# A selective scan's units in a new order: five pairs of states by tokens, three by rows, and the carry by DMA

## The chip, the cores and the metric

The kernel runs on one core of a Trainium2 chip. A NeuronCore has four engines that compute, each with its own instruction stream: TensorE (PE) for matrix products, VectorE (DVE), ScalarE (ACT) and GpSimd (POOL). A fifth, SyncE (SP), only issues DMAs. They meet through semaphores. The metric is the device time of one execution in microseconds; lower is better. Unless another length is named, a "group" and a "unit" below are those of the second layer's scan.

## The reference, cut to what matters

Two layers of a state-space image model on 64 x 64 positions with 96 channels, each `x + conv_ref(groupnorm(x))`. The change lies in the second layer, in its selective scan: 4 directions, 192 inner channels, 16 states, 4096 positions.

```python
A = -jnp.exp(A_logs)
def step(h, t):
    u_t, d_t, B_t, C_t = t
    h = h * jnp.exp(d_t[..., None] * A[None]) + (d_t * u_t)[..., None] * B_t[:, :, None, :]
    y = jnp.einsum('bkdn,bkn->bkd', h, C_t)
    return (h, y)
```

For every channel d and state n this is a first-order recurrence along the positions: a = exp(dt x A), b = dt x u x B, h = a x h + b, and y sums h x C over the states. Before it stand projections, a depthwise convolution and a softplus for dt; after it a layer norm, a gate and an output projection.

## The kernel before, in words

**Groups.** Layer 2's scan is the function `scans`. Its work is cut into 16 groups: two pairings of directions, two directions, four chunks of 1024 positions. A group needs `dt` and `du` (dt times u) of its chunk, B and C.

**Units.** A group has 24 units: three blocks T of 64 channels by eight pairs m of states. A tile of a unit has 128 partitions (two states by 64 channels) and 1024 positions. A unit goes through these steps, each a small function:

- `stage_a` (ScalarE): a = exp(dt x A), into a pool of three buffers
- b, in PSUM, in one of two ways. By rows: `stage_B` (TensorE) spreads two rows of B over the partitions by two matmuls, and `stage_b` (VectorE) multiplies the result by `du`. By tokens: ScalarE has multiplied `du`, transposed so that positions lie on partitions, by B as a scale for each partition (`product`, 16 operations for a pair m, shared by the three T, into seven buffers `bT`); `stage_t` (TensorE) turns the products back with eight transposes, and VectorE has nothing to multiply
- `stage_s` (VectorE): the scan itself, one instruction, into `h`, a pool of three buffers
- `stage_k`: the last element of each partition of h is copied to `carry`, from which the next chunk's unit starts. It is left out for a direction's last chunk
- `stage_c` (GpSimd): hc = h x C; C's two rows come from DRAM, spread over 64 partitions each by two DMAs into `cb` (`fetch_c`, three buffers)
- `stage_r` (TensorE): sums hc over the states into PSUM, on top of y; `stage_y` (ScalarE) copies y out after the last pair

Before the change the even pairs go by rows and the odd by tokens, and the units alternate: row unit, token unit, row unit. The row units' b lies in PSUM tile `b0`, the token units' in `b1`.

**The order.** The last loop of `scans` writes the program out unit by unit. In its iteration j it emits b of unit j+1, a of unit j+2, the product b x du and the scan of unit j, the sum of unit j-3, carry and C product of unit j-1. Everything emitted through `pe`, `act`, `dve`, `pool` and `sp` keeps this order on its engine. Tiles are handed over by semaphores: whoever writes a buffer again waits for its last reader.

**Preludes.** What group k+1 needs is made while group k runs, by the list `steps`: each entry has a slot (a unit's number, counted from the group's own start, so slots below 0 lie in the group before) and is emitted at the end of the iteration that the slot falls in. `delta(T)` is the softplus for dt (ten steps), `project`, `first_part`, `less_part`, `next_part`, `rows` and `tokens_B` make B and C, `tokens_du` transposes du, `spread(T)` copies dt and du to both halves of the partitions with eight DMAs on SP. `turns` says how many of the 16 products of each token pair are emitted in which unit.

**SP's queue** carries, in program order: the DMAs of `fetch_c`, `spread` and `rows`. Each of its DMAs signals one of eight semaphores in turn, and an issue waits until the DMA eight issues earlier has landed.

In the profile all instructions that go through `Ordered` have the line of its `issue` (L653 before), so they are told apart by their tiles.

Of the kernel before, what the change touches and what calls it, by code (L numbers as in the profile page):

```python
# [8 lines left out]
F32 = mybir.dt.float32  # L9
# [12 lines left out]
NP = NS // 2  # L22
RK = 6
TC = 1024
# [19 lines left out]
def two_ss2d_layers(  # L44
# [592 lines left out]
    def scans(weights):  # L637

        xw, dwb, _ = weights
        pinned = []

# [16 lines left out]
        with ExitStack() as sc:  # L661
# [5 lines left out]
            am = decays(weights[2])  # L667
            carry = pre.tile([128, 3, NP], F32, name="carry")
            PER = 3 * NP
            LAG = 3  # L670
            halves = [slice(0, HT), slice(HT, TC)]
            state = [{} for _ in GROUPS]
# [24 lines left out]
            def prelude(k):  # L697
# [81 lines left out]
                def delta(T):  # L779

                    def begin():
                        ps = me["pd", T] = spare(f"pd{k}_{T}", tags[2 + T])
                        for h, half in enumerate(HALF):
                            pe.matmul(
                                ps[half], dwb[p][96 : NC + 1, d, T, half],
                                xd[96 : NC + 1, halves[h]], start=True, stop=True,
                            )

                    def new(nm, own):
                        t = me[nm, T] = pre.tile(  # L790
                            [128, HT], F32, tag=f"{nm}{T}" if own else nm, name=f"{nm}{k}_{T}"
                        )
                        return t

                    def absolute():
                        act.activation(new("su", True), me["pd", T], AF.Abs)

                    def positive():
                        act.activation(new("sp", True), me["pd", T], AF.Relu)

                    def exponent():
                        act.activation(new("w", False), me["su", T], AF.Exp, scale=-1.0)

                    def logarithm():
                        act.activation(new("ln", False), me["w", T], AF.Ln, bias=one)

                    def plus():
                        act.activation(me["pd", T], me["w", T], AF.Identity, bias=one)

                    def missed():  # L810

                        dve.scalar_tensor_tensor(
                            me["w", T], me.pop(("pd", T)), -1.0, me["w", T], ALU.add, ALU.subtract
                        )

                    def found():
                        add_engine.tensor_sub(me["ln", T], me["ln", T], me["w", T])

                    def whole():
                        add_engine.tensor_add(me["sp", T], me["sp", T], me["ln", T])  # L820

                    def times():
                        add_engine.tensor_mul(me["su", T], me["sp", T], chunk(u[T], c))

                    return [
                        begin, absolute, positive, exponent, logarithm, plus, missed,
                        found, whole, times,
                    ]

                def spread(T):  # L830
                    for nm, of in (("dt", "sp"), ("du", "su")):
                        t = me[nm, T] = pre.tile(
                            [128, TC], F32, tag=f"{nm}{T}", name=f"{nm}{k}_{T}"
                        )
                        both(t.rearrange("p (h t) -> p h t", h=2), me[of, T], sp)
# [4 lines left out]
                for h in range(2):  # L840
# [10 lines left out]
                        (o + 3 + late, lambda h=h: next_part(1, h)),  # L851
                    ]
                steps += [
                    (-9, rows), (-6.8, tokens_B), (-5.95, tokens_B_out),

                    *zip((-1.5, -1, -1, 0, 1, 1, 2, 3, 4, 5), delta(0)),
                    *zip((2.5, 3, 3, 4, 5, 5, 6, 7, 8, 9), delta(1)),
                    *zip((6.5, 7, 7, 8, 9, 9, 10, 11, 12, 13), delta(2)),
                ]
                steps += [(18.5 + e, lambda e=e: tokens_du(e)) for e in range(4)]  # L860
                steps += [(19 + e, lambda e=e: tokens_du_out(e)) for e in range(4)]
                steps += [(18 + 2 * T, lambda T=T: spread(T)) for T in range(3)]


                turns = (
                    (19, (4, 4, 4, 4)), (PER, (3, 1, 5, 1, 3, 3)), (PER + 6, (4, 2, 3, 1, 3, 3)),
                    (PER + 12, (2, 3, 3, 2, 3, 3)),
                )
                for i, (slot, counts) in enumerate(turns):
                    todo = [(e, h, n) for e in range(4) for h in range(2) for n in range(2)]  # L870
# [8 lines left out]
            def product(k, i, e, h, n):  # L879


                me = state[k]
                if (h, n) == (0, 0):
                    me["bT", i, e] = mn.tile(
                        [128, 2, 3, 2, 64], F32, tag="bT", name=f"bT{k}_{i}{e}", bufs=7
                    )
                q = 2 * (2 * i + 1) + n
                act.mul(
                    me["bT", i, e][:, h, :, n, :], me["duT", e][:, h],
                    me["BT"][:, e + 4 * h, q : q + 1],  # L890
                )

            units = [
                (k, T, 2 * i + odd)
                for k in range(len(GROUPS)) for i in range(NP // 2) for T in range(3)
                for odd in range(2)
            ]
            N = len(units)
            live = {}

# [8 lines left out]
            def stage_B(j):  # L909

                k, T, m = units[j]
                ps = live["b", j] = pps.tile([128, TC], F32, tag="b0", name=f"b{j}")
                for s in halves:
                    pe.matmul(
                        ps[:, s], pick(GROUPS[k][1], m), state[k]["B3"][:, s], start=True, stop=True
                    )

            def stage_t(j):

                k, T, m = units[j]  # L920
                ps = live["b", j] = pps.tile([128, TC], F32, tag="b1", name=f"b{j}")
                for e in range(4):
                    t = state[k]["bT", m // 2, e]
                    for h in range(2):
                        q = e + 4 * h
                        pe.transpose(
                            ps[:, 128 * q : 128 * (q + 1)],
                            t[:, h, T].rearrange("p n c -> p (n c)"), ident,
                        )
# [23 lines left out]
            def stage_k(j):  # L953
                k, T, m = units[j]
                p, d, c = GROUPS[k]
                if c != (NCH - 1 if d == 0 else 0):
                    act.copy(carry[:, T, m : m + 1], along(d, live["h", j])[:, TC - 1 : TC])

            def stage_c(j):
                k, T, m = units[j]  # L960
# [3 lines left out]
            def stage_r(j):  # L964


                k, T, m = units[j]
                p, d, c = GROUPS[k]
                v = live.pop(("hc", j))
                if m == 0:  # L970
                    ps = live["y", T] = pps.tile([128, HT], F32, tag=f"y{T}", name=f"ys{j}")

                    parts = [(chunk(y[T], c), lambda s: s)] if (p, d) != (1, 0) else views(y[T], c)
                    for q, (view, f) in enumerate(parts):
                        pe.matmul(f(ps), ident, view, start=(q == 0), stop=False)
                ps = live["y", T]
                for h, half in enumerate(HALF):
                    pe.matmul(
                        ps[half], fold[:, 0:64], v[:, halves[h]], start=False, stop=(m == NP - 1)
                    )  # L980

            def stage_y(j):
                k, T, m = units[j]
                p, d, c = GROUPS[k]
                if m == NP - 1:
                    ps = live.pop(("y", T))
                    parts = [(chunk(y[T], c), lambda s: s)] if (p, d) != (1, 1) else views(y[T], c)
                    for view, f in parts:
                        act.copy(view, f(ps))
# [10 lines left out]
            def unit(step, at):  # L1000
                if 0 <= at < N:
                    step(at)

            for j in range(-5, N + LAG + 2):
                if j == 0:
                    pinned.append(True)

                for ahead, odd in ((4, 0), (1, 1)):
                    k, i = divmod(j + ahead, PER)
                    if i % 6 == 0 and 0 <= k < len(GROUPS):  # L1010
                        fetch_c(k, i // 3 + odd)
                unit(stage_B if j % 2 else stage_t, j + 1)
                unit(stage_a, j + 2)
                if j % 2 == 0:
                    unit(stage_b, j)
                unit(stage_r, j - LAG)
                unit(stage_s, j)
                unit(stage_k, j - 1)
                unit(stage_y, j - LAG - 1)
                unit(stage_c, j - 1)  # L1020
                while steps and steps[0][0] < j + 1:
                    steps.pop(0)[2]()

# [339 lines left out]
```

## Time and profile before

| | us |
|---|---|
| median of 3 runs | 1578.04 (1571.17 to 1579.99) |
| the profiled execution | 1590.44 |
| its span, first to last instruction | 1588.6 |
| scans of layer 2, first to last | 321.2 to 1536.3 |
| VectorE busy | 1354.7 |
| TensorE busy | 1286.9 |
| ScalarE busy | 1198.7 |
| GpSimd busy | 1092.4 |

Times of the profile are of one execution, so a sum made from it stands against 1590.44 and its span, not against the median. A line for a group of instructions gives the engine, the operation, the tiles written and read, partitions x elements, the count, then the busy time and the mean duration of one, then the idle time of the engine just before such instructions and what ended it. Busy time is a union, so overlapping instructions count once. "SPq" is a DMA issue on SyncE's queue. In a timeline the columns are start, length in us, engine, line, operation, tiles and count.

### The profile page before, as it was taken

Reading aid. Unit: us, or ns where it says so; the run is one execution under the profiler, and the core shown is the slowest. Engines: PE = TensorE matmul, PEld = TensorE weight load, DVE = VectorE, ACT = ScalarE, POOL = GpSimd, SP = SyncE. Lnnn points to the kernel's source line nnn. Section 1 sums busy time; section 2 is a strip of 40 time slices with the busy share of each in tenths; the row PEclk is TensorE's granted clock in tenths of the full one; section 3 lists DMA queues with packets and bytes.
Section 4 is the critical chain, followed back from the end, with each engine's and each line's share of the span. In section 5 each row is a group of like instructions: output and inputs, shape, how many; then the busy total and the mean of one; then the engine's idle time right before and its main releaser. Section 6 shows DMA issues by size and latency. Waiting matters only on the chain.

```text
span 1588.6 us, 17352 instructions
## 1 busy us (share of the span) xinstructions
PE 1286.9 (81%) x5158; PEld 515.7 (32%) x5158; DVE 1354.7 (85%) x935; ACT 1198.7 (75%) x2474; POOL 1092.4 (69%) x577
## 2 busy tenths in 40 slices
PE   5963779769898889897988888898988888876768
PEld 3432424223333323232323333333333233322223
DVE  6836489339999998999899999989999999999976
ACT  3444234759988897989799889989897989897733
POOL 0021100019898988898898979898989898999860
PEclk8975689859999998999899899989999998999999
DMA  4033330432626262644435262615252635436223
GB/s 108 20 97 85 85 88 1 132 70 53 135 55 141 64 143 53 135 91 97 104 84 136 67 134 66 135 53 135 55 133 67 147 73 116 108 80 137 76 82 90
DMA packets 84307, 148.10 MB, mean 93 GB/s; under 512 B 31676, under 2 KB 35068, under 8 KB 84108
## 3 DMA queue, kind: packets, MB, share of 16 engines
q1 hardware_dynamic: 80428, 143.76, 37.9%
q10 hardware_dynamic: 3776, 3.15, 0.9%
q8 instruction: 42, 0.69, 0.2%
q14 instruction: 61, 0.50, 0.1%
HBM read 80.85 MB, written 12.13 MB: 59 GB/s over the span
## 4 chain that ended last, share of the span: by engine, by line
DVE 23%; PE 20%; issue 16%; ACT 13%; DMA 7%; SPq 5%; POOL 4%; DVEq 0%; ACTq 0%; POOLq 0%
DVE h L653 15%; PE ys L653 5%; DVE b L653 5%; SPq L653 5%; ACT a L653 5%; PE pj L653 5%; PE b L653 4%; DMA cb<-C 3%; ACT bT L653 3%; POOL hc L653 3%; PE cp L1120 2%; PE pd L653 2%; DMA du<-su 2%; DMA xT<-xs 1%; DVE w L653 1%
## 5 line engine op out<-in xcount | busy, mean ns | idle before, releaser
L653 POOL TENSOR_TENSOR hc<-h,cb 128x1024 f32<-128x1024 f32 x384 | 903.4, 2366 | 232.7 <-DMA dt<-sp 96.0
L653 DVE TENSOR_TENSOR_SCAN h<-a,carry,b 128x1024 f32<-128x1024 f32 x288 | 665.3, 2337 | 44.2 <-PE b L653 21.8
L653 ACT ACTIVATE a<-dt,am 128x1024 f32<-128x1024 f32 x384 | 438.6, 1143 | 95.7 <-DVE h L653 93.9
L653 PE MATMUL ys<-hc,fold 128*64 128x512 f32 x1536 | 435.6, 647 | 3.5 <-POOL hc L653 3.5
L653 ACT ACTIVATE bT<-duT,BT 128x192 f32<-128x192 f32 x1024 | 392.2, 445 | 12.1 <-PE b L653 10.1
L653 PE MATMUL b<-ident,bT 128*128 128x128 f32 x1536 | 226.7, 292 | 35.0 <-DVE h L653 30.0
L653 DVE TENSOR_TENSOR b<-b,du 128x1024 f32<-128x1024 f32 x192 | 232.4, 1210 | 11.3 <-PE b L653 11.1
L653 DVE TENSOR_TENSOR_SCAN h<-a,b 128x1024 f32<-128x1024 f32 x96 | 216.2, 2277 | 22.0 <-PE b L653 15.7
L653 PEld LDWEIGHTS b<-ident,bT 128*128 128x128 f32 x1536 | 179.9, 149 | 163.9 <-DVE h L653 101.1
L653 PE MATMUL b<-B,selh 96*128 96x512 bf16 x384 | 125.0, 409 | 96.3 <-DVE h L653 95.6
L653 PEld LDWEIGHTS ys<-hc,fold 128*64 128x64 f32 x1536 | 79.0, 140 | 144.0 <-issue 99.8
L653 PE MATMUL pj<-u,xw 64*124 64x512 f32 x192 | 103.9, 691 | 2.4 <-ACT sz L1102 1.8
L653 PE MATMUL pd<-xd,dwb 29*64 29x512 f32 x192 | 62.1, 716 | 53.9 <-DVE w L653 47.2
L653 PEld LDWEIGHTS <-selh 96*128 96x128 bf16 x384 | 26.8, 100 | 225.9 <-DVE h L653 126.2
L1143 DVE SCALAR_TENSOR_TENSOR acc<-pad,v,acc 128x1052 f32<-128x1052 f32 x64 | 79.6, 1307 | 0.2
L653 POOL TENSOR_TENSOR ln<-ln,w 128x512 f32<-128x512 f32 x45 | 57.5, 1278 | 14.8 <-DVE w L653 14.8
L653 PE MATMUL ys<-y,ident 128*128 128x512 f32 (+1 forms) x120 | 64.9, 648 | 0.0
L653 ACT CAST B<-pj 96x512 bf16<-96x512 f32 (+2 forms) x96 | 55.1, 575 | 12.4 <-PE pj L653 12.2
L1120 PE MATMUL cp<-pad,diag 128*128 128x512 f32 x144 | 62.3, 593 | 0.0
L653 POOL TENSOR_TENSOR sp<-sp,ln 128x512 f32<-128x512 f32 x45 | 57.4, 1276 | 0.0
L653 POOL TENSOR_TENSOR su<-sp,u 128x512 f32<-128x512 f32 x45 | 57.4, 1275 | 0.0
L653 PEld LDWEIGHTS pj<-u,xw 64*124 64x124 f32 x192 | 36.2, 203 | 64.7 <-issue 46.5
(163 smaller groups left out, 1147.5 us busy)
## 6 DMA issues: line engine op xcount, KB each, us to landing
cb<-C SPq DMA_DIRECT2D x256, 256.0 KB
dt<-sp SPq DMA_DIRECT2D x192, 128.0 KB
du<-su SPq DMA_DIRECT2D x192, 128.0 KB
szd<-sz SPq DMA_DIRECT2D x24, 256.0 KB
szt<-szd SPq DMA_DIRECT2D x24, 256.0 KB
xT<-xs SPq DMA_DIRECT2D x8, 384.0 KB
xs<-xT SPq DMA_DIRECT2D x1, 1536.0 KB
xs<-xT SPq DMA_DIRECT2D x8, 192.0 KB
```

The lines of the kernel that those rows point to most:

```text
L653: ins = op(*args, **more)
L1120: nc.tensor.matmul(ps.rearrange("p (r w) -> p r w", w=HW), diag[:, k, :], pad[b][:, c, i : i + SR, j : j + HW], start=(k == 0), stop=(k == ...
L1143: nc.vector.scalar_tensor_tensor(acc, src, wk, acc, ALU.mult, ALU.add)
```

## The change

Three parts, all in `scans`.

1. Five of the eight pairs of states go by tokens (m = 3 to 7) and three by rows (m = 0 to 2). The units follow the pattern `ORDER`, R for a row unit and T for a token unit: `RTTT`, then `RTRTT` four times; within each kind they go pair by pair, and T by T. b's PSUM tile is now by the unit's parity (`b{j % 2}`), not by its kind.
2. `stage_k` moves the carry with a DMA on SP in place of ScalarE's copy.
3. What depends on the order follows it: the first and last unit of each T for y (`begins`, `ends`), the units in which C is fetched (`fetches`), the slots of the deltas' later steps, of `tokens_B_out` and of `spread`, and the products for each unit (`turns`).

```diff
+            ORDER = "RTTT" + 4 * "RTRTT"
+            by_rows, by_tokens = range(3), range(3, NP)
...
-                    (-9, rows), (-6.8, tokens_B), (-5.95, tokens_B_out),
-                    *zip((-1.5, -1, -1, 0, 1, 1, 2, 3, 4, 5), delta(0)),
-                    *zip((2.5, 3, 3, 4, 5, 5, 6, 7, 8, 9), delta(1)),
-                    *zip((6.5, 7, 7, 8, 9, 9, 10, 11, 12, 13), delta(2)),
+                    (-9, rows), (-6.8, tokens_B), (-5.85, tokens_B_out),
+                    *zip((-1.5, -1, -1, 0, 1, 1, 2, 3, 4, 6), delta(0)),
+                    *zip((2.5, 3, 3, 4, 5, 5, 6, 8, 9, 11), delta(1)),
+                    *zip((6.5, 7, 7, 8, 9, 9, 10, 12, 14, 16), delta(2)),
...
-                steps += [(18 + 2 * T, lambda T=T: spread(T)) for T in range(3)]
+                steps += [(slot, lambda T=T: spread(T)) for T, slot in enumerate((19.5, 21.2, 22.2))]
...
-                    (19, (4, 4, 4, 4)), (PER, (3, 1, 5, 1, 3, 3)), (PER + 6, (4, 2, 3, 1, 3, 3)),
-                    (PER + 12, (2, 3, 3, 2, 3, 3)),
+                    (19, (4, 4, 4, 4)), (PER - 1, (2, 5, 2, 3, 4)), (PER + 4, (5, 2, 5, 2, 2)),
+                    (PER + 8, (1, 5, 2, 4, 2, 2)), (PER + 13, (1, 5, 2, 4, 2, 2)),
...
-                q = 2 * (2 * i + 1) + n
+                q = 2 * by_tokens[i] + n
...
-            units = [
-                (k, T, 2 * i + odd)
-                for k in range(len(GROUPS)) for i in range(NP // 2) for T in range(3)
-                for odd in range(2)
-            ]
+            kinds = {"R": iter([(T, m) for m in by_rows for T in range(3)]),
+                     "T": iter([(T, m) for m in by_tokens for T in range(3)])}
+            group = [next(kinds[kind]) for kind in ORDER]
+            begins = {T: [t for t, m in group].index(T) for T in range(3)}
+            ends = {T: PER - 1 - [t for t, m in group[::-1]].index(T) for T in range(3)}
+            units = [(k, T, m) for k in range(len(GROUPS)) for T, m in group]
...
-                ps = live["b", j] = pps.tile([128, TC], F32, tag="b0", name=f"b{j}")
+                ps = live["b", j] = pps.tile([128, TC], F32, tag=f"b{j % 2}", name=f"b{j}")
...
-                    act.copy(carry[:, T, m : m + 1], along(d, live["h", j])[:, TC - 1 : TC])
+                    sp.dma_start(
+                        out=carry[:, T, m : m + 1], in_=along(d, live["h", j])[:, TC - 1 : TC]
+                    )
...
+            R, S = by_rows, by_tokens
+            fetches = {
+                20: [(5, S[0])], 23: [(1, R[0])], 1: [(0, S[1])], 5: [(0, S[2])], 8: [(0, R[1])],
+                10: [(0, S[3])], 15: [(0, R[2])], 16: [(0, S[4])],
+            }
             for j in range(-5, N + LAG + 2):
...
-                for ahead, odd in ((4, 0), (1, 1)):
-                    k, i = divmod(j + ahead, PER)
-                    if i % 6 == 0 and 0 <= k < len(GROUPS):
-                        fetch_c(k, i // 3 + odd)
-                unit(stage_B if j % 2 else stage_t, j + 1)
+                unit(stage_B if of_rows(j + 1) else stage_t, j + 1)
                 unit(stage_a, j + 2)
-                if j % 2 == 0:
+                if of_rows(j):
                     unit(stage_b, j)
...
                 unit(stage_c, j - 1)
+                for ahead, m in fetches.get(j % PER, ()):
+                    if 0 <= j + ahead < N:
+                        fetch_c((j + ahead) // PER, m)
                 while steps and steps[0][0] < j + 1:
                     steps.pop(0)[2]()
```

In `fetches`, the number before the colon is the unit within the group, and `(5, S[0])` means: C of the first token pair, for the group of the unit five on.

## The prediction

> **What bounds the kernel now.** I read the sums of the stretch that holds groups 1 to 14 first, then the costliest groups of the page, then the waits of VectorE and GpSimd, and last the timeline of SP's queue around one group boundary.
>
> ```profile
> core 0: us, PE busy (x) PEld busy (x) DVE busy (x) ACT busy (x) POOL busy (x), PEclk, DMA share, GB/s
> 421.40:1465.00 1043.60, 884.07 (x3766) 338.25 (x3765) 982.30 (x545) 921.82 (x1947) 937.70 (x462) 0.93 0.43 100
> ```
>
> Fourteen groups in 1043.6 us are 74.5 us each. VectorE is busy 94% of that; ScalarE, GpSimd and TensorE stand at 88, 90 and 85%, so none of them has much room.
>
> ```profile
> L653 POOL TENSOR_TENSOR hc<-h,cb 128x1024 f32<-128x1024 f32 x384 | 903.4, 2366 | 232.7 <-DMA dt<-sp 96.0
> L653 DVE TENSOR_TENSOR_SCAN h<-a,carry,b 128x1024 f32<-128x1024 f32 x288 | 665.3, 2337 | 44.2 <-PE b L653 21.8
> L653 ACT ACTIVATE bT<-duT,BT 128x192 f32<-128x192 f32 x1024 | 392.2, 445 | 12.1 <-PE b L653 10.1
> L653 DVE TENSOR_TENSOR b<-b,du 128x1024 f32<-128x1024 f32 x192 | 232.4, 1210 | 11.3 <-PE b L653 11.1
> ```
>
> In the trace a scan that follows a scan starts 2.26 us after it; where a product b lies between, the distance is 3.58, so a product costs 1.32. A group has 12 units of each kind and three short VectorE operations of 0.58: 12 x 2.26 + 12 x 3.58 + 1.7 = 71.8 us. The measured 74.7 (mean of groups 1 to 14, scan to scan) is 2.9 above it. What ends that idle time, in the stretch 450 to 1450:
>
> ```profile
> DVE h L653 <- PE b L653: 25.4, 20, 2.5
> DVE b L653 <- PE b L653: 9.7, 16, 0.9
> ```
>
> So VectorE bounds the scans and TensorE is the only engine that makes it wait. Now SP's queue at a boundary, in the timeline (start, length, what, count):
>
> ```profile
> 702.64 1.08 SPq L653 DMA_DIRECT2D cb<-C  x2
> 703.77 2.52 SPq L653 DMA_DIRECT2D dt<-sp  x4
> 706.39 2.47 SPq L653 DMA_DIRECT2D du<-su  x4
> 708.95 1.18 SPq L653 DMA_DIRECT2D cb<-C  x2
> 710.23 2.47 SPq L653 DMA_DIRECT2D dt<-sp  x4
> 712.80 2.47 SPq L653 DMA_DIRECT2D du<-su  x4
> 715.36 2.46 SPq L653 DMA_DIRECT2D dt<-sp  x4
> 717.92 2.47 SPq L653 DMA_DIRECT2D du<-su  x4
> 720.49 42.60 SPq L653 DMA_DIRECT2D cb<-C  x12
> ```
>
> SP issues without a gap for 19 us, 0.64 us for each DMA. What comes at the end of that row is late already: GpSimd waits for cb of unit 25.
>
> ```profile
> 726.39 2.36 POOL L653 TENSOR_TENSOR hc<-h,cb 128x1024 f32<-128x1024 f32 x1 [1.19 <-DMA cb<-C]
> ```
>
> **What the Trainium skill says.** "DMA: Bandwidth & Descriptors", section "Anatomy of one DMA — SWDGE (gpsimd) path", says that a DMA has about 2 us of fixed time, and that a wait for a semaphore happens on the issuing sequencer, not in the DMA engines. The trace agrees: C<-xd, alone on its queue, lands 1.9 us after its issue, and its wait for ACT's xd holds SP. Its "Rules for kernel authors" say that issuing from several engines saves only the sequencer's issue time; here that time, 0.64 us, is what counts. "VectorE: DVE Perf Modes", section "The TRN2 errata — SBUF-src ops pay a fixed extra latency per instruction", prices a ScalarE operation at 224 cycles and one per element, at 1.2 GHz: 347 ns for 192 elements. The trace has bT operations 346 ns apart, so the 445 of the page is a latency. "Perfetto Trace Analysis", section "Identifying the Most-Contended Engine", calls matmul busy time a bad measure of headroom; here eight transposes of 292 ns take 1.16 us together, so I follow TensorE's chain instead of its 85%.
>
> **The change part by part.** VectorE: 3 of 24 units go from rows to tokens, so 48 products less in the 16 groups, 48 x 1.32 = 63 us, 3.96 a group; its floor falls from 71.8 to 67.9.
>
> ScalarE: 16 bT operations more a group, 16 x 0.346 = +5.5; the carry copies go, which follow each other 0.081 apart (18 a group on average), -1.4. By such distances its work goes from 64.2 to 68.3 us a group, level with VectorE's. Its busiest stretch, units 23 to 10 of the next group, holds 36.0 us of work (12 a x 1.04, 40 bT, 15 operations of the three deltas with 8.2, three y with 1.4) beside 34.1 of VectorE: 2 us that the two units' lead of a and any stall of VectorE there can cover.
>
> TensorE: eight transposes take 1.16 us a unit (187.2/161 in the window's groups), two matmuls with B3 0.65 (104.4/161): +1.5 a group. But b of unit j+1 has to wait for the scan of j-1, and two banks stay two banks, so runs of T matter. I walked both orders unit by unit: TensorE does b of j+1, ys of j-3 (1.14) and the prelude of that unit (pj 3.2 at units 11 and 14, pd 1.2, y's start 1.38, less 0.43, tu 0.55); each unit's b starts at the later of the end of that and the scan of j-1. For the kernel before the walk gives 2.2 us of stall a group (2.9 measured). For the new order it gives 0.9 at unit 8, 0.8 at 13 and 1.85 at 16: 3.5. (The last: TensorE comes free at 43.2 us into the group; b of 15 to 44.4, ys to 45.5, pj to 48.7, b of 16 to 49.35, and scan 15 has ended at 47.5.) So this takes back 1.3, and a group without anything else gains 3.96 - 1.3 = 2.6.
>
> GpSimd's operations stay; its work is 24 x 2.32 + 9 x 1.23 = 66.8 a group, so it can hardly catch up once it is late. The moved slots of the deltas spread its three-operation chains over T and R units; I price that at nothing, since the trace shows GpSimd behind a scan by 0.1 to 1.9 us and two units of h cover it; without that cover a 1.23 operation would show.
>
> SP: 288 DMAs of 128 elements of 4 bytes, 24 in each of 12 groups (a last chunk hands nothing on). The trace has no such DMA in the scans; the loads of the start with 64 rows and short runs take 0.6 to 0.65 of SP and land after 1.9 to 2.2. Bounds: 0.31 (C<-xd) to 0.65 to issue, 1.9 to 5.4 to land (the late cb behind the full row above); I take 0.64, as two waits stand before each, and 2.4 to 4. Away from the boundary a carry is free: its h is written again by the scan three units on, at least 4.5 us later. What it is put into at the boundary is the point. Carry of unit j waits at SP's head for the scan of j, and the spreads (eight DMAs each) and cb stand behind it in program order. With 0 at the end of scan 18 and VectorE unhindered, scans 19 to 27 end at 3.6, 5.8, 9.4, 11.7, 13.9, 17.5, 19.8, 22.0, 24.3. SP:
> - carry 18 at 0.1; spread 0 0.7 to 5.9; in the kernel before its first DMA stood at -2.2 to -1.7, since it waited only for ScalarE's last a on dt
> - carry 19 to 6.5, cb of unit 25 to 7.7, carry 20 to 8.3, spread 1 to 13.4
> - carry 21 to 14.0, lands about 17; scan 24 writes over its h and would start at 15.3
> - spread 2 to 19.1, carry 22 to 19.7, lands 21.5 to 23; scan 25 would start at 17.5
> - cb of unit 24 (two DMAs) to 21, lands about 24.5 (4.1 after its second issue, as cb's median here). Before, the DMA in this place served unit 25.
>
> The product hc of unit 24 then ends near 26.8, and scan 27, which needs its h, would have started at 22.0: 4.7 us late. The carry alone makes scan 25 4 to 5 late; the two overlap. TensorE's walk starts from scan 25, so its stalls come on top; GpSimd goes on just ahead of VectorE's needs (within 1 us to unit 9), so I expect no second loss and no recovery. With the bounds, the lateness is 2.3 (issue 0.31, land 1.9, cb 3.5) to 6.1 (cb 5.4).
>
> Sum against the profiled execution: 12 groups x (4.7 - 2.6) = +25; groups 3, 7 and 11, without carries, 3 x -2.6 = -8; the last group, without a prelude, -4; the start, where four more bT come ahead of a long chain of ScalarE, +1.4. +15 us on the span of 1588.6, that is near 1604; the profiled run is 1590.4, 12 above the median, so against the median: 1578 + 15 = 1593.
>
> **Rivals.** The break-even lateness is 2.6 + 10.4/12 = 3.5 us.
> - SP's row is hidden and the kernel is faster. If scans 19 to 24 are themselves later (ScalarE has 11.7 us of work for units 19 to 22, as much as VectorE), or a carry issues in 0.3 us, lateness falls to 2: 12 x -0.6 - 10.4 = -18, 1560; with none at all 1536. For it: VectorE's saving is sure, and SP's row before the change cost GpSimd 1 us and VectorE nothing. Against: SP's head now waits for scans, and 31 DMAs stand ahead of the cb that one unit needs a unit earlier. It decides below 3.5 us.
> - TensorE's runs of T cost more than the walk says: it granted 0.93 of its clock here, and transposes for a T after a T have only one scan, 2.26 us, to run in beside 1.14 of ys. With 1.6 us more in 15 groups 1617, with 3.2 1641. Against: the walk was short by only 0.7 before.
> - No change that can be told: lateness of 2.8 to 4.2.
>
> **Numbers.** The main case slower, 0.40; within 0.5% (about what a measurement of this kernel can tell from no change) 0.17; SP hidden and faster 0.28; TensorE dearer 0.15. Slower is 0.55 together. The main case's own range, from the bounds of lateness, is 1564 to 1610; with a tenth of the chance left below, among the faster cases, and a tenth above, in TensorE's, 1552 to 1624.
>
> **What would show it.** VectorE's busy time in the scans 63 us down; bT 1280 times; the scans of units 24, 25 and 27 waiting for DMA carry or for GpSimd, GpSimd's hc of unit 24 waiting 5 us or more for cb, groups of 77 us with carries and 72 without. It is wrong if SP's row ends before unit 24's scan, if carries issue in 0.3 us, or if groups with and without carries take the same time; then SP is not the cause. If hc waits for cb but scans 24 to 27 do not wait, two units of h cover it.

## The result, and the profile after

The changed kernel takes 1625.51 us in the median (1621.19 to 1627.07, four runs), the kernel before beside it 1579.01: a ratio of 1.0285, 95% interval 1.0219 to 1.035. So it is slower, as forecast, but by 46 us where the forecast was 15, and just outside its range (1552 to 1624). The two profiled executions lie nearer: spans of 1619.4 and 1588.6 us, +31. The profile of before was one of its slower runs and that of after is its fastest. The granted clock of TensorE is nearly the same in both, 0.893 before and 0.899 after.

From the page, the costliest groups of the kernel after:

```profile
L654 POOL TENSOR_TENSOR hc<-h,cb 128x1024 f32<-128x1024 f32 x384 | 901.9, 2372 | 267.7 <-DMA carry<-h 143.9
L654 DVE TENSOR_TENSOR_SCAN h<-a,carry,b 128x1024 f32<-128x1024 f32 x288 | 664.2, 2337 | 104.8 <-DMA carry<-h 44.6
L654 ACT ACTIVATE bT<-duT,BT 128x192 f32<-128x192 f32 x1280 | 482.0, 445 | 2.0
L654 DVE TENSOR_TENSOR b<-b,du 128x1024 f32<-128x1024 f32 x144 | 174.8, 1214 | 20.0 <-PE b L654 20.0
```

The work moved as meant: the products b fell from 232.4 to 174.8 us, and bT grew from 392.2 to 482.0, where 88.6 more were forecast (16 x 16 x 0.346). But the idle time before the scans went from 44.2 to 104.8 us, and a releaser stands there that the kernel before didn't have: the landing of a carry. VectorE's waits in the stretch 450 to 1450:

```profile
DVE h L654 <- DMA carry<-h: 34.7, 21, 4.2
DVE h L654 <- PE b L654: 23.6, 18, 2.6
DVE b L654 <- PE b L654: 17.4, 18, 1.4
DVE h L654 <- ACT bT L654: 10.1, 5, 3.5
DVE h L654 <- ACT a L654: 8.7, 18, 1.3
```

The waits for TensorE's b went from 35.1 to 41.0 us in sum. The carry is new, and the waits for ScalarE's bT and a grew from 2.0 to 18.8. SP's timeline at one boundary (start, length, what, count; the scan of unit 18 ended at 705.0):

```profile
705.61 2.48 SPq L654 DMA_DIRECT2D dt<-sp  x4
708.13 2.54 SPq L654 DMA_DIRECT2D du<-su  x4
710.77 0.54 SPq L654 DMA_DIRECT2D carry<-h  x1
711.41 1.19 SPq L654 DMA_DIRECT2D cb<-C  x2
712.69 0.55 SPq L654 DMA_DIRECT2D carry<-h  x1
713.33 2.48 SPq L654 DMA_DIRECT2D dt<-sp  x4
715.86 2.52 SPq L654 DMA_DIRECT2D du<-su  x4
718.47 0.54 SPq L654 DMA_DIRECT2D carry<-h  x1
719.11 2.47 SPq L654 DMA_DIRECT2D dt<-sp  x4
721.63 2.53 SPq L654 DMA_DIRECT2D du<-su  x4
724.26 0.54 SPq L654 DMA_DIRECT2D carry<-h  x1
724.90 1.19 SPq L654 DMA_DIRECT2D cb<-C  x2
```

This is the row (the DMAs that SP issues one behind the other at a group's end) that the prediction wrote down: the carry of unit 22 issues 19.2 us after the end of scan 18 (19.1 there), C of unit 24 has its second issue 20.5 us after it (20.4). VectorE and then GpSimd in the same place:

```profile
721.13 2.35 DVE L654 TENSOR_TENSOR_SCAN h<-a,carry,b 128x1024 f32<-128x1024 f32 x1 [1.08 <-DMA carry<-h]
726.23 2.35 DVE L654 TENSOR_TENSOR_SCAN h<-a,carry,b 128x1024 f32<-128x1024 f32 x1 [2.76 <-DMA carry<-h]
730.16 2.35 DVE L654 TENSOR_TENSOR_SCAN h<-a,carry,b 128x1024 f32<-128x1024 f32 x1 [1.58 <-DMA carry<-h]
```

```profile
714.56 7.03 POOL L654 TENSOR_TENSOR hc<-h,cb 128x1024 f32<-128x1024 f32 x3 [1.09 <-DVE h L654]
730.20 7.00 POOL L654 TENSOR_TENSOR hc<-h,cb 128x1024 f32<-128x1024 f32 x3 [8.61 <-DMA carry<-h]
```

Scans 24, 25 and 26 each wait for a carry. GpSimd stands idle for 8.6 us: by the trace's semaphores C of unit 24 landed at 729.7, and the carry that the profile names is one of those that landed just behind it. Then come three products in a row: GpSimd starts that of unit 24 when VectorE is already scanning unit 26.

That lateness goes on into the group. ScalarE's waits:

```profile
ACT w L654 <- POOL ln L654: 30.8, 18, 3.2
ACT ln L654 <- POOL sp L654: 8.9, 17, 0.8
```

The kernel before has next to nothing in these two lines:

```profile
ACT ln L653 <- POOL sp L653: 2.0, 3, 0.8
ACT w L653 <- POOL ln L653: 0.9, 2, 0.5
```

One of these waits, in ScalarE's timeline after the change:

```profile
749.41 1.14 ACT L654 ACTIVATE a<-dt,am 128x1024 f32<-128x1024 f32 x1
753.75 0.63 ACT L654 ACTIVATE w<-su 128x512 f32<-128x512 f32 x1 [3.20 <-POOL ln L654]
```

Scan to scan, a group that starts behind one with carries takes 78.3 us (77.2 if it has no carries itself; 78.0 for both), one that starts behind a group without carries 75.1; before, the mean was 74.7. The difference between the two kinds says less than it seems to. A group behind one without carries begins a direction, its scans start from 0, and such a scan takes 2277 ns where one with a carry takes 2337: 1.4 us in 24 units. The kernel before has such a difference too (75.4 and 72.2), with no carry on SP.

### The profile page after: what moved, and what is told of

Same layout as the page of the kernel before. It is cut to its first block, busy times and chain, and to the rows that moved or that the text cites. A ratio compares the mean times of both kernels' runs of the same rounds, so it can differ in the third digit from the quotient of the medians.

```text
span 1619.4 us, 18617 instructions
## 1 busy us (share of the span) xinstructions
PE 1293.2 (80%) x5446; PEld 545.2 (34%) x5446; DVE 1302.3 (80%) x887; ACT 1256.5 (78%) x2442; POOL 1091.3 (67%) x577
## 4 chain that ended last, share of the span: by engine, by line
ACT 24%; DVE 17%; PE 14%; issue 13%; SPq 8%; DMA 7%; POOL 6%; DVEq 0%; POOLq 0%; ACTq 0%
DVE h L654 13%; ACT bT L654 8%; ACT a L654 8%; SPq L654 7%; POOL hc L654 4%; PE pj L654 4%; PE ys L654 3%; ACT B L654 2%; PE b L654 2%; DMA carry<-h 2%; PE cp L1133 2%; DVE b L654 2%; DMA dt<-sp 2%; PE pd L654 1%; DMA xT<-xs 1%
## 5 line engine op out<-in xcount | busy, mean ns | idle before, releaser
L654 DVE TENSOR_TENSOR_SCAN h<-a,carry,b 128x1024 f32<-128x1024 f32 x288 | 664.2, 2337 | 104.8 <-DMA carry<-h 44.6
L654 ACT ACTIVATE bT<-duT,BT 128x192 f32<-128x192 f32 x1280 | 482.0, 445 | 2.0
L654 PE MATMUL ys<-hc,fold 128*64 128x512 f32 x1536 | 446.3, 662 | 2.2 <-POOL hc L654 2.2
L654 PE MATMUL b<-ident,bT 128*128 128x128 f32 x1920 | 283.0, 291 | 149.4 <-DVE h L654 101.0
L654 PEld LDWEIGHTS b<-ident,bT 128*128 128x128 f32 x1920 | 224.5, 148 | 317.6 <-DVE h L654 131.3
L654 DVE TENSOR_TENSOR_SCAN h<-a,b 128x1024 f32<-128x1024 f32 x96 | 215.6, 2277 | 32.9 <-PE b L654 20.0
L654 DVE TENSOR_TENSOR b<-b,du 128x1024 f32<-128x1024 f32 x144 | 174.8, 1214 | 20.0 <-PE b L654 20.0
L654 PE MATMUL b<-B,selh 96*128 96x512 bf16 x288 | 95.3, 415 | 17.3 <-DVE h L654 16.1
L654 PE MATMUL pj<-u,xw 64*124 64x512 f32 x192 | 91.5, 621 | 5.7 <-ACT B L654 3.9
L1133 PE MATMUL cp<-pad,diag 128*128 128x512 f32 x144 | 62.3, 593 | 0.0
L654 PEld LDWEIGHTS <-selh 96*128 96x128 bf16 x288 | 19.6, 99 | 123.0 <-issue 96.7
L654 ACT ACTIVATE w<-su 128x512 f32<-128x512 f32 x48 | 30.2, 629 | 38.2 <-POOL ln L654 36.6
L654 DVE SCALAR_TENSOR_TENSOR w<-pd,w 128x512 f32<-128x512 f32 x48 | 32.5, 676 | 33.5 <-ACT pd L654 32.9
```

The source lines that it names most:

```text
L654: ins = op(*args, **more)
L1133: nc.tensor.matmul(ps.rearrange("p (r w) -> p r w", w=HW), diag[:, k, :], pad[b][:, c, i : i + SR, j : j + HW], start=(k == 0), stop=(k == ...
```

## The experiments

Theory A is the prediction's: at the boundary between two groups SP's row makes carries and C late. Theory B is that runs of token units on TensorE cost the time; theory C that ScalarE does. The runs e1 to e4 shared a chip and the runs of the kernel before, and so did e5 to e8, e9 to e11, e12 to e14, and e15 to e17. From chip to chip the kernel before had medians of 1572 to 1577. So differences of some us between these sets mean little, and the ratios are given beside the medians.

| run | median, us | ratio to before (95%) |
|---|---|---|
| e1 all carries by ScalarE | 1579.8 | 1.0027 (1.0011 to 1.0043) |
| e2 before, carry by DMA | 1691.1 | 1.0708 (1.0666 to 1.0751) |
| e3 C one unit earlier | 1626.9 | 1.0330 (1.0309 to 1.0352) |
| e4 carries of units 18 to 23 by ScalarE | 1572.5 | 0.9979 (0.9962 to 0.9996) |
| e5 = e3 and e4 | 1537.0 | 0.9729 (0.9674 to 0.9784) |
| e6 = e4, w twice | 1577.0 | 1.0001 (0.9985 to 1.0018) |
| e7 = e5, w and ln twice | 1528.2 | 0.9674 (0.9621 to 0.9728) |
| e8 = e2, fetch last | 1639.6 | 1.0387 (1.0322 to 1.0453) |
| e9 = e5, half the sums | 1536.6 | 0.9777 (0.9703 to 0.9851) |
| e10 = e5, deltas' old slots | 1524.3 | 0.9695 (0.9622 to 0.9768) |
| e11 carries on ScalarE's queue | 1587.8 | 1.0092 (1.0069 to 1.0115) |
| e12 = e5, products once a pair | 1500.6 | 0.9552 (0.9512 to 0.9593) |
| e13 = e7 and e10 | 1529.6 | 0.9727 (0.9680 to 0.9773) |
| e14 after, deltas' old slots | 1600.9 | 1.0194 (1.0143 to 1.0245) |
| e15 after, two slots back | 1596.9 | 1.0131 (1.0111 to 1.0152) |
| e16 after, w and ln twice | 1593.3 | 1.0121 (1.0091 to 1.0151) |
| e17 after again | 1622.8 | 1.0260 (1.0198 to 1.0322) |

**The carry's way, e1 and e4.** In e1 only the copy comes back; in e4 only where the row is full:

```diff
-                    sp.dma_start(
-                        out=carry[:, T, m : m + 1], in_=along(d, live["h", j])[:, TC - 1 : TC]
-                    )
+                    if j % PER >= PER - 6:
+                        act.copy(carry[:, T, m : m + 1], along(d, live["h", j])[:, TC - 1 : TC])
+                    else:
+                        sp.dma_start(...)
```

> The changed kernel with the carry copied by ScalarE again, nothing else undone. Theory A (SP's row at the group boundary: carries wait for scans at its head, spreads and C's DMAs stand behind them): the boundary stalls of the groups after a group with carries (units 0 to 3: 3.5, 1.4, 0.6 us more than their nominal distances) shrink to what the groups after a group without carries have; those are 3.2 us shorter, so 12 x 3.2 = 39 us off, about 1587, ratio to before near 1.005. Theory B (runs of T on TensorE are the cause): the time stays within 8 us of the changed kernel, near 1622, as TensorE's work is untouched. Theory C (ScalarE is the new bound): slower than the changed kernel, as 288 copies come back, +23 us.

> The changed kernel with only the carries of units 18 to 23 copied by ScalarE; the other 18 of a group stay DMAs. Theory A: the harm of the DMAs is all at the boundary, so this is within 8 us of the run with all carries on ScalarE, near 1587. If DMAs hurt everywhere (by landing late under C's transfers, or by holding SP for later fetches), it gains a quarter of that at most, near 1615.

e1 gives back nearly all of the loss, so B is out as its cause: TensorE's order is untouched. Nor is theory C seen here: the 288 copies that come back to ScalarE cost nothing that shows. e4 is no slower than e1 but 0.5% faster: 18 of 24 carries by DMA do no harm that shows, and the six at the boundary do all of it.

**Part one alone, e2 and e8.** The kernel before with the DMA carry; in e8 C's fetch is also moved to the end of the iteration, behind the carry, where the changed kernel has it.

```diff
-                    act.copy(carry[:, T, m : m + 1], along(d, live["h", j])[:, TC - 1 : TC])
+                    sp.dma_start(
+                        out=carry[:, T, m : m + 1], in_=along(d, live["h", j])[:, TC - 1 : TC]
+                    )
```

> The kernel before with only the carry moved to a DMA; order, pairs and slots as before. Theory A: SP's row of 24 spread DMAs now has carries in it that wait for scans, so carries of units 18 to 22 land 1 to 3 us after the scan that writes over their h could start: about 3 us in each of 12 groups, ratio 1.02. Theory B: no more than 1.002, since the order of units is unchanged; ScalarE even loses 23 us of copies that it had room for.

> The kernel before with the carry by DMA, as in e2, but C's fetch emitted after the carry in each iteration, as the changed kernel has it. In e2 scans 7, 13, 19 start 1 to 2 us late, each two units after a fetch that waits for GpSimd at SP's head with carries behind it. If that is the difference between the 2% that theory A gave and the 7% measured, this is at 1.02 to 1.035. If the row at the boundary alone makes 7%, it stays above 1.06.

A's walk for the old order gave 2%, e2 measured 7%. With the fetch last it is 3.9%, a little above the 2 to 3.5% that were expected, and its scans away from the boundary are no longer late. So 3 of the 7% are the same mechanism in another place: a fetch that waits for GpSimd at SP's head, with carries behind it. The 3.9% that stay are nearly twice the walk's 2%: here too the walk made the boundary too cheap.

**C of unit 24, e3 and e5.** e3 is the changed kernel with this line, e5 is e4 with it:

```diff
-                20: [(5, S[0])], 23: [(1, R[0])], 1: [(0, S[1])],
+                20: [(5, S[0])], 22: [(2, R[0])], 1: [(0, S[1])],
```

> The changed kernel with C of the next group's first unit fetched one unit earlier, so that it stands on SP ahead of the third spread. Splits the boundary. If the late cb alone makes the boundary (GpSimd at unit 24, then the scan of unit 27), 4 to 5 us in 15 groups go, near 1560. If the carries behind the third spread hold scans 25 and 26 by themselves, as theory A has it, they still stand behind it: no more than 1 to 1.5 us a group, 1603 to 1620.

> The kernel of e4 (carries of units 18 to 23 by ScalarE) and, as in e3, C of the next group's first unit fetched one unit earlier, ahead of the third spread. With the carries out of SP's row, theory A leaves one lateness there: hc of unit 24 starts 4 us after its scan, waits for cb, and GpSimd's softplus operations behind it come late. If so, hc of unit 24 starts within 0.3 us of its scan's end and 2 to 3.3 us a group go (3.3 is what the groups after a group without carries gained in e3): 15 x 2.5 = 38 us below e4, near 1535, ratio 0.974. If two units of h hide the late cb, less than 8 us, near 1567.

Alone it gains nothing (1.0330 beside 1.0285): the carries of units 22 and 23 still stand behind the third spread, and now behind C too. The groups show both halves of this. Behind a group without carries they take 71.8 us in e3 and 75.1 in the changed kernel; behind one with carries 78.4 and 78.0. With the carries of the boundary gone, C one unit earlier is worth 2.5%, 36 us. Two waits stood side by side, and the late C shows its price only where the late carries are gone; they show theirs with C still late (e4). GpSimd's waits for cb in the stretch 450 to 1450, of e4 and of e5:

```profile
POOL hc L654 <- DMA cb<-C: 60.2, 13, 5.1
```

```profile
POOL hc L654 <- DMA cb<-C: 2.9, 4, 1.4
```

e5 is already 2.7% faster than the kernel before.

**SP's row or the DMA itself, e11.** The changed kernel with `act.dma_start` in place of `sp.dma_start` for the carry.

> The changed kernel with its carry DMAs issued from ScalarE's queue. If the place in SP's row makes the carries late (theory A), the boundary is as in e1 with cb late alone, and what is left is the price of an issue on ScalarE: at 0.08 us (as the copy) near 1580, at 0.3 us 18 x 0.22 = 4 us a carry group of ScalarE's work, 1590 to 1620. If a DMA of 128 short elements is slow wherever it is issued, the time stays at 1622 or above with scans 24 to 26 waiting for carries.

1.0092: no scan waits for a carry in its profile any more, so it was the place in SP's row and not the form of the transfer. C is late as in e1 (GpSimd waits 62.3 us for cb, 53.0 in e1).

**What a group still loses in e5: TensorE or ScalarE, e9 and e12.** Both leave part of the computation out or change it. In e9:

```diff
                 for h, half in enumerate(HALF):
+                    if h and j % PER not in (begins[T], ends[T]):
+                        continue
...
```

In e12 one operation writes both states of a pair, with a read that repeats:

```diff
+                if n:
+                    return
                 act.mul(
-                    me["bT", i, e][:, h, :, n, :], me["duT", e][:, h],
+                    me["bT", i, e][:, h],
+                    me["duT", e][:, h].unsqueeze(2).to_broadcast([128, 3, 2, 64]),
...
```

> The kernel of e5 with the second half of the sums over states (stage_r, the second 512 positions) left out for all units but the first and last of each block, so TensorE has about 10 us less of 68 in a group; y is incomplete. In e5 a group takes 71.7 us, 3.8 above VectorE's nominal 67.9; the walk along TensorE gave 3.5. If TensorE's chain makes those, 2.5 to 3.5 us a group go: 1537 - 15 x 3 = 1492. If ScalarE (68.3 of work a group) makes them, less than 10 us, above 1527.

> The kernel of e5 with ScalarE's token products made once for both states of a pair (one operation of 384 elements in place of two of 192, so the second state has the first one's B): about 0.51 us in place of 0.69 by the distances seen, 7.4 us of ScalarE's 68.3 less in a group, all else the same. If ScalarE makes the 3.8 us that a group of e5 takes above VectorE's nominal 67.9, 2 to 3 us of them go: near 1500. If it is the coupling of VectorE with TensorE and GpSimd, less than 10 us: above 1527.

In e9 576 of the 1536 sums over states are gone, by the walk's 1.14 us for the four sums of a unit about 10 us of TensorE's work per group (36 sums), and the time stays: 1536.6 beside 1537.0. In e12 7.4 us of ScalarE's work per group are gone and the time falls by 36 us (28 by the ratios), as theory C has it. VectorE's waits for TensorE's b in the stretch 450 to 1450, of e5 and of e12:

```profile
DVE b L654 <- PE b L654: 16.2, 16, 1.4
DVE h L654 <- PE b L654: 15.6, 22, 1.2
```

```profile
DVE b L654 <- PE b L654: 0.7, 2, 0.4
DVE h L654 <- PE b L654: 0.3, 2, 0.2
```

A profile names who ended a wait last, and that was TensorE. But TensorE itself waited for ScalarE's products: 44.6 us for bT in the same stretch of e5, 0.9 in the kernel before. With fewer sums (e9) VectorE still waits 33.9 us for b; with shorter products these waits are gone. The same stretch of 1000 us in e5, e9 and e12 (busy time and count of PE, PEld, DVE, ACT, POOL):

```profile
421.00:1421.00 1000.00, 854.19 (x4017) 352.21 (x4016) 934.12 (x504) 969.41 (x1973) 938.71 (x462) 0.98 0.45 104
```

```profile
421.00:1421.00 1000.00, 855.16 (x3521) 351.71 (x3520) 934.19 (x504) 968.85 (x1974) 937.38 (x463) 0.98 0.45 105
```

```profile
421.00:1421.00 1000.00, 874.24 (x4146) 359.87 (x4144) 963.67 (x520) 900.16 (x1452) 964.16 (x474) 0.99 0.46 106
```

ScalarE is busy 97% in e5 and 90% in e12, while VectorE and GpSimd go from 93 and 94% to 96%; TensorE's 85% doesn't move when an eighth of its matmuls go. A group takes 71.6 us in e5, 71.6 in e9 and 69.3 in e12. So of the 3.7 us that e5 has above VectorE's nominal 67.9, ScalarE's products make at least 2.3; the other 1.4 are not taken apart here.

**The deltas' slots and the buffers of w and ln, e6, e7, e10, e13 to e17.** ScalarE writes w and ln of each block into one buffer; GpSimd reads the block before from it.

```diff
-                        [128, HT], F32, tag=f"{nm}{T}" if own else nm, name=f"{nm}{k}_{T}"
+                        [128, HT], F32, tag=f"{nm}{T}" if own else nm, name=f"{nm}{k}_{T}",
+                        bufs=2 if nm in ("w", "ln") else 1,
...
```

(e6 has w alone. In e6, e7, e13 and e16 hc has three buffers in place of four to make room.) e10 and e14 have the three `delta` lines of the kernel before; e15 only this:

```diff
-                    *zip((2.5, 3, 3, 4, 5, 5, 6, 8, 9, 11), delta(1)),
+                    *zip((2.5, 3, 3, 4, 5, 5, 6, 7, 8, 11), delta(1)),
```

> The kernel of e4 with two buffers for w, the softplus' intermediate that GpSimd reads last and ScalarE writes again for the next block (room for it from hc, three buffers in place of four). In e4 ScalarE waits 35 us for GpSimd's ln there, up to 3.2 us at a time, and scans 10 start 1.6 to 2.6 us late. If that wait makes them late, about 1.5 us a group go: 22 us, near 1550. If the lateness is GpSimd's own and only moves to the next wait (ln for GpSimd's sp, or hc), less than 6 us.

> e5 and e6 together, with two buffers of ln as well. If GpSimd's lateness from the boundary is what ScalarE waits for at w, e5 has removed it, and this is within 6 us of e5. If the wait at w is of the order itself (the three GpSimd operations of a block strung over row units), it adds to e5: another 20 us, near 1515.

> The kernel of e5 with the slots of the deltas' last three steps as in the kernel before (7, 8, 9 and 11, 12, 13 for blocks 1 and 2, 5 for block 0). The prediction priced these moves at nothing: within 8 us of e5, 1529 to 1545. If they matter, GpSimd's three operations of 1.23 us in a row, two of them beside scans that follow scans, make hc late by more than h's two units cover: 1 to 2 us a group, 1552 to 1567.

> The kernel of e5 with the deltas' old slots (e10) and two buffers for w and ln (e7, hc with three). If both took away the same wait, ScalarE's for GpSimd at w and ln, this is within 5 us of e10, 1519 to 1529. If they are separate, near 1515.

e6 gains nothing: the wait for w went away and one for ln came, 50.7 us in its stretch (8.0 in e4). e7 has both twice and gains 9 us on e5, between the less than 6 and the 20 of its two expectations; e10 with the old slots gains 13 (the intervals of their ratios overlap; spans of 1535.1, 1525.4 and 1524.2 say the same). Together (e13) they give no more than one of them, which fits that they remove one wait. e10 was a miss: it was expected at the price of nothing, or else slower, and it is faster.

> The changed kernel with only the deltas' old slots. In e10 they took 13 us off, 0.9 a group. If the slots harm the changed kernel as much, 1612, ratio 1.02. If its groups are held by the boundary and by GpSimd's lateness from there, the earlier slots put ScalarE's w less far behind GpSimd's ln and may give more, 1590 to 1605; or nothing, 1620 to 1627, if the boundary hides them.

> The changed kernel with only two slots moved back: GpSimd's first two steps of block 1's softplus at 7 and 8 as before, not 8 and 9. ScalarE writes w and ln of block 2 at 8 and 9, into the same single buffers, so with the new slots it waits for GpSimd's step of the same iteration. If that wait is the harm of the moved slots, this gets most of what e14 got: 12 to 20 us under e17. If it is the order of GpSimd's work in general, less than 6 us.

> The changed kernel, slots as changed, with two buffers for w and ln (hc with three). Takes the same wait away in another way: 12 to 25 us under e17 if the wait for w and ln is the harm; if GpSimd's lateness finds the next wait (as with w alone in e6, where the wait moved to ln), less than 6 us.

> The changed kernel itself on the same chip, as the measure for the two: ratio 1.0285 to the kernel before as measured, 1.022 to 1.035.

On one chip, the changed kernel took 1622.8 us, with two slots moved back 1596.9, with the slots as changed but w and ln twice 1593.3. So 26 of the 46 us (20 by the ratios of e17 and e15) hang on GpSimd's first two steps of block 1, more than the 12 to 20 expected. e14, which moves all these slots back, was measured on another chip and lies 22 us under e17 (10 by the ratios). These two steps used to be emitted at units 7 and 8; the change puts them at 8 and 9, the units in which ScalarE writes w and ln of block 2 into the same buffers. ScalarE then waits for a step of the same iteration on an engine that in the stretch shown is one to two units behind VectorE's scans. The two harms feed each other: this wait comes to 35.1 us in e4, where C is late, and to 4.6 in e5, where it isn't. In e15 the line shown above for the changed kernel is:

```profile
ACT w L654 <- POOL ln L654: 7.2, 10, 0.9
```

## Why the prediction was wrong in size

The direction and the main mechanism, SP's row, were right. Two terms of the sum failed: the moved slots, which it put at nothing, and the lateness at the boundary, which it made too small.

- **The moved slots, "I price that at nothing": this step failed most.** It was argued from VectorE's cover (two units of h). The one who waits is ScalarE, through single buffers of w and ln that the step didn't ask about. Measured: 26 us between e17 and e15 (20 by the ratios), and w and ln twice takes the same wait away (e16).
- **The price of the boundary, 4.7 us in 12 groups, was too low.** e14 and e10 differ in this alone: the carries of units 18 to 23 and the place of C. They are 77 us apart (on different chips, with the kernel before at 1571.8 and 1574.3, so it is good to a few us); 56 were forecast. Group by group, e14 is 5.2 us longer than e10 behind groups with carries, near the 4.7, and 3.7 us longer behind the three groups without, which were taken as free: C of unit 24 is late there as well. One term inside the 4.7 was left out too: the carry of unit 23 stands behind C of unit 24 and lands about 4 us after its issue, so scan 26 waits as well, and scan 27 starts 28.0 us after scan 18 where 26.8 were forecast.
- **SP's row: right in mechanism and place.** In the boundary shown the issue times agree within 0.3 us. Scan 24 was to wait for a carry that lands at about 17 us after scan 18 and starts at 16.1; scan 25 was to wait until 21.5 to 23 and starts at 21.2.
- **VectorE's saving and ScalarE's load: right.** 232.4 to 174.8 us and 392.2 to 482.0. A kernel with the order and without both the boundary's lateness and the moved slots (e10) is 50 us under the kernel before by medians; 42 were forecast.
- **The sum.** The forecast was -42 + 56 + 0 = +15, rounded. Measured it is about -50 + 77 + 20 to 26, that is 47 to 53, where the medians say 46: the pieces come from different chips, and the last two don't simply add, so they fit to some us.
- **The stalls inside a group, 3.5 us, were put down to TensorE: size right, cause wrong.** e5 has 3.2 to 4.0. That the walk along TensorE's chain gave as much is luck: of its places, units 8, 13 and 16, only the last shows more than 0.5 us in e5, 1.2. e9 removed part of that chain for nothing, and e12 shows ScalarE in at least 2.3 of it. The prediction's own sums, ScalarE 68.3 beside VectorE 67.9, had hinted at it.
- **The rivals.** SP's row hidden: refuted, as e14 and e10 show 5.2 us of lateness where break-even was 3.5. The 1536 that the prediction wrote for no lateness at all is the 1537.0 of e5, partly by luck, since e5 still holds 13 us of the slots' wait (e10). TensorE dearer: refuted by e1, which keeps TensorE's order at 1.0027, and by e9.
- **The signs.** bT ran 1280 times, scans 24 and 25 waited for carries and hc of unit 24 for C. Scan 27 was to wait too; in the boundary shown it doesn't, since the wait came at scan 26. Groups of 77 us with carries and 72 without were expected; 78.0 and 75.1 came. That sign was weak in any case, as the kernel before has 75.4 and 72.2 (see above).
- **From profile to median** the prediction moved its sum by the 12 us that the profiled run of before lay above the median. The kernel before scatters (1559 to 1593 in the 32 runs beside e15), so that offset isn't a constant: +31 between the profiles is +46 between the medians.

## What to carry to other kernels

In this kernel a small DMA did no harm except where others stood before it on its queue. So list the queue in program order, with what each issue waits for, and ask for every buffer that a DMA reads when the buffer is written next. When two late transfers stand side by side, taking one away can show nothing (e3); take both away before judging either. When steps of another engine are moved, look for the single buffer that a third engine writes after them. And a wait that is put down to one engine can be made by the engine that this one waited for: shorten the work of each and see which shortens the wait.

## What the runs showed of the hardware

- In the changed kernel a carry, 128 elements of 4 bytes, has a median of 0.50 us on SP's queue and lands 1.85 us after its issue in the median; in the boundary shown it is 2.5 us for the carry of unit 21, behind a spread, and 3.9 for that of unit 23, behind the two transfers of C. The 2 us that the prediction quotes are given, in the section that it cites, for DMAs that GpSimd issues. SP issues these, so the figure rests on the trace.
- Issued from ScalarE's queue (e11) it takes 0.47 us. In one place of its timeline that hides behind the operation that is running: the next a follows two bT after 0.70 us, twice 0.35, with an issue in between. Over the whole kernel e11 is still 8 us slower than e1, which ran on another chip; why was not taken apart.
- A ScalarE operation of 384 elements with a repeated read follows another after 0.507 us (e12). That is what the Trainium skill's "VectorE: DVE Perf Modes", section "The TRN2 errata — SBUF-src ops pay a fixed extra latency per instruction", prices: 224 + 384 cycles at 1.2 GHz.
- TensorE's busy time did not follow its load here: 854 and 855 us of 1000 with 4017 and 3521 matmuls (e5 and e9).
